# Blocks 2 to 4 of a modulated feed-forward kernel: the first wide product on two levels in all three, modulation taken up early in each second stage, late inner sums on GpSimd

## The chip, the cores and the metric

The kernel runs on one core of one Trainium2 chip. The metric is the device time of one execution in microseconds (us); less is better. Beside it stands a profile: one execution with the start and length of every instruction on the engines TensorE (PE, with its weight loads as PEld), VectorE (DVE), ScalarE (ACT), GpSimd (POOL) and SyncE (SP, which only issues DMAs here).

## The reference, cut to what matters

```python
q_emb = relu(q @ W3 + b3)                      # (64 batches, 512)
v_sum = sum(v, axis=1, keepdims=True)          # v = x: (64, 64, 512)
m = (n * v + v_sum) * q_emb[:, None, :]        # the modulation, n = 64
y = relu(m @ W2 + b2)                          # first wide product, 512 x 512
out = x + (y @ W_base + b_base) + (y @ A_s) @ B_s + routed(y)
# routed: softmax over 6 experts, the best two weigh (y @ A_r) before B_r
```

Everything is float32. There are 4096 rows (64 batches of 64 rows) of 512 features.

## The kernel before

**Tiling.** The rows are cut into four blocks, `k` = 0 to 3 in the code, blocks 1 to 4 in words. A block has 16 batches (1024 rows). Features lie on the 128 partitions in four chunks (`NC` = 4, visited as `CHUNKS` = 0, 2, 1, 3); rows lie along the free axis in two halves of `TB` = 512.

**Stages of a block.** A first stage computes `y` (first wide product, relu). Then come 64 narrow matmuls into `ph` (the low-rank factors and the router, L814), and four `row_sums` of `y` on DVE into the tile `sy`. Then `second` does the second wide product, the gate, the routed part and the output DMAs.

**Wide products with fewer multiplications.** A wide product is a 2 x 2 block product (features by row halves) done with seven half-size products instead of eight (`product`, L168): sums and differences of the weights (`weight_sums`) and of the rows (`row_sums`, L252) go in, and the results are linked by ACT copies from PSUM bank to PSUM bank ("seeds") and by DVE additions. Block 1 does its first product partly directly (`first_mixed`). Block 2 uses seven products on one level (`first_seven`, L429: 14 calls of `product`, of two 128x512 matmuls each). Blocks 3 and 4 use the identity on two levels (`first_inner`, L462): each of the seven outer products is again done with seven inner ones, 49 matmuls of 128x256. For that the inner weight sums `inner_t` (12 DVE instructions, L161 to L164) and the inner row sums of `prepare_inner` are needed: "first" (four of 128x256, outer product 1), "sums" (four of 128x1024, outer products 5, 6, 7, 3) and "late" (four of 128x512, outer products 2 and 4), all on DVE.

**The order inside `first_inner`.** The outer products run as steps t = 0 to 6 in the order (1, 5, 6, 7, 2, 3, 4). `q(n, t)` is the n-th inner matmul of step t. `open_banks(t)` takes two of the six PSUM banks of the pool "pp". `seed_y`, `seed_z` are ACT copies that later matmuls add to; `take_1`, `take_21`, `take_22`, `take_u`, `take_w5` read the banks out, on DVE (L476) or ACT. The additions marked L579 and L582 are done on GpSimd. `q(4, t)` writes the half bank that `take_22(t)` has to have read.

**The modulation.** For each chunk, `sums(c)` on DVE makes `nq` (L203), the sums over the rows (`TENSOR_REDUCE`, L204) and their product with `q` (L205). Then 16 ACT instructions (`batch`, L209) modulate the chunk in place, so 64 a block. This work for block `k + 1` is done during block `k`.

**The queue `behind`.** The program order of each engine is written out by hand; engines run in that order and wait for each other by semaphores. `prepare(k + 1)` lays the modulation, the row sums and the inner sums of the next block into the list `behind` in small units (two `batch` each, some with a DVE step), and `fill(n)` emits the next n units at that point. In `second`, `share()` is called nine times and spreads what is left evenly. The `sums(c)` of block 4 and `inner_t` are made, beside those of block 3, during block 2 (`k == NB - 2` in `prepare`).

Of the kernel before, what the change touches and what calls it, by code (L numbers as in the profile page):

```python
# [19 lines left out]
TB = 512  # L20
# [16 lines left out]
def adaln_ffn(ctx: ExitStack, tc: tile.TileContext, xa, x0, x1, head, w3, w2, wb, a, bcat, br, outT):  # L37
# [155 lines left out]
    def modulate(k):  # L193


        vs[k] = v = xs[k]
        vsum = small.tile([P, NC, BB], F32, tag=f"vsum{k}", name=f"vsum_{k}")
        nq = small.tile([P, NC, BB], F32, tag=f"nq{k}", name=f"nq_{k}")
# [12 lines left out]
        return ({c: lambda c=c: sums(c) for c in CHUNKS},  # L211
                {c: [lambda c=c, b=b: batch(c, b) for b in range(BB)] for c in CHUNKS})
# [62 lines left out]
    modulation = {}  # L275

    def prepare(k):

        if k == NB:
            return
        if k not in modulation:
            modulation[k] = modulate(k)
        sums, batches = modulation[k]
        ss[k], row_steps = row_sums(vs[k], "s")
        early, late = row_steps(slice(0, 1)), row_steps(slice(1, 2))
        units = [] if k == NB - 1 else [[sums[CHUNKS[0]]]]
        for i, c in enumerate(CHUNKS):
            for b in range(0, BB, 2):  # L290
                unit = batches[c][b : b + 2]
                if b == 0 and i + 1 < NC and k < NB - 1:
                    unit.insert(0, sums[CHUNKS[i + 1]])
                if i == NC - 1 and b % 4 == 2:
                    unit.append(early[b // 4])
                units.append(unit)
        if k == NB - 2:
            modulation[k + 1] = modulate(k + 1)
            for n, step in enumerate(list(modulation[k + 1][0].values()) + inner_steps):
                units[1 + n].append(step)  # L300
        behind.extend(units + [[step] for step in late])
        if k > 1:
            behind.extend([step] for step in prepare_inner(k))

    def prepare_inner(k):
# [6 lines left out]

        def late_places():
            late = mid.tile([P, 4, KH, TB], F32, tag="sy", name=f"inner_late_{k}").rearrange("p n k t -> p (n k t)")
            s["late"] = late[:, : 8 * R2].rearrange("p (n o t) -> p n o t", n=4, o=2)
            s["e3"] = late[:, 8 * R2 : 12 * R2].rearrange("p (j t) -> p j t", j=KH)

        def steps(g, a):
            return [
                lambda: nc.vector.tensor_tensor(s[g][:, 0], a(0, 1), a(1, 1), ALU.add),  # L320
                lambda: nc.vector.tensor_tensor(s[g][:, 1], s[g][:, 0], a(0, 0), ALU.subtract),
                lambda: nc.vector.tensor_tensor(s[g][:, 2], a(0, 0), a(0, 1), ALU.subtract),
                lambda: nc.vector.tensor_tensor(s[g][:, 3], a(1, 0), s[g][:, 1], ALU.subtract),
            ]

        late = [late_places] + steps("late", lambda c, r: vs[k][:, KH + c, :, ts(r, R2)])
        where = {1: ("first", 0), 2: ("late", 0), 4: ("late", 1), 5: ("sums", 0), 6: ("sums", 1), 7: ("sums", 2),
                 3: ("sums", 3)}
# [8 lines left out]

        inner[k] = dict(s=side, e3=lambda: s["e3"], late=late)
        first = steps("first", lambda c, r: vs[k][:, c, 0, ts(r, R2)].unsqueeze(1))
# [6 lines left out]
    def first_mixed(y):  # L346
# [81 lines left out]

    def first_seven(k, y):  # L429

        s = ss[k]
        prepare(k + 1)
        pairs = temps(k)
        for j in range(KH):
            f1, f2 = j, KH + j
            bank = lambda n: ps_p.tile([P, TB], F32, tag="pp", name=f"y{n}_{k}_{j}")
            temp = lambda n: pairs[n][:, j]
            px, py, pw, pz = bank("x"), bank("y"), bank("w"), bank("z")
            u, r, r2 = temp("u"), temp("u22"), temp("u12")
            product(px, 1, j, t2, s)  # L440
            nc.scalar.copy(py, px)
            product(pw, 5, j, t2, s)
            nc.scalar.copy(r, pw)
            product(py, 6, j, t2, s, start=False)
            nc.scalar.copy(pz, py)
            product(px, 2, j, t2, s, start=False)
            nc.scalar.copy(u, py)
            fill(2)
            relu(y, f1, 0, px)
            product(pz, 7, j, t2, s, start=False)  # L450
            nc.vector.tensor_tensor(r, pz, r, ALU.add)
            fill(2)
            relu(y, f2, 1, r)
            product(pw, 3, j, t2, s, start=False)
            nc.vector.tensor_tensor(r2, pw, u, ALU.add)
            fill(2)
            relu(y, f2, 0, r2)
            product(pz, 4, j, t2, s, start=False)
            relu(y, f1, 1, pz)
            fill(2)  # L460

    def first_inner(k, y):  # L462


        order = (1, 5, 6, 7, 2, 3, 4)
        for step in inner[k]["late"]:
            step()
        prepare(k + 1)
        t_side, s_side = inner_t, inner[k]["s"]
        pairs, e3 = temps(k), inner[k]["e3"]()  # L470
        p1, p5, u, v7 = (pairs[n] for n in ("u", "u22", "u21", "u12"))
# [84 lines left out]
        take_22(0)  # L556
        q(2, 1)
        for t in range(2, 7):
            open_banks(t)
# [92 lines left out]
    def second(k, y, ph, res):  # L652
# [47 lines left out]

        left = [9]

        def share():
            fill(-(-len(behind) // left[0]))
            left[0] -= 1

# [84 lines left out]
    for k in range(NB):  # L791
        y = mid.tile([P, NC, 2, TB], F32, tag="y", name=f"y_{k}")
        rest = None
        if k == 0:
            first_mixed(y)
        elif k == 1:
            first_seven(k, y)
        else:
            rest = first_inner(k, y)
# [73 lines left out]
```

## Time and profile before

| | |
|---|---|
| median of 3 runs | 263.54 us (263.38 to 265.14) |
| the profiled execution: its time, its span | 263.01 us, 261.2 us |
| granted TensorE clock | 1.0 |
| busy: PE, DVE, ACT, POOL | 98%, 67%, 51%, 6% of the span |

The span goes from the first to the last instruction; some 1.8 us of the profiled execution lie around it. Times below are us from the start of the span. In a listing of instructions in order of time the columns are: start, length, engine, line, operation, output <- inputs, shapes, count, and in brackets the idle time before it with what ended it. Lengths of neighbours can overlap[...]; the distance from start to start is what an instruction costs its queue. The stages stand in time as follows, read from the chain of work that ended last (the chain is 93% PE): first stage of block 1 to 33.66, `ph` and `second` to 72.59; block 2: first stage to 97.52, `ph` to 104.66, `second` to 136.46; block 3: first stage and `ph` to 165.62, `second` to 197.43; block 4: first stage and `ph` to 226.18, `second` to 258.1.

### The profile page before, as it was taken

What the parts mean: (1) busy time and instruction counts of PE and PEld (TensorE: products, weight loads), DVE (VectorE), ACT (ScalarE), POOL (GpSimd) and SP (SyncE); (2) the same over time, 40 slices, a digit from 0 to 9 for tenths busy, and PEclk for the clock granted to TensorE, in tenths of its full rate; (3) what the DMA queues carried; (4) which work ended last, traced back from release to release, by engine and by line L of the source; (5) the groups of instructions that cost most, each with busy time, mean ns of one, the idle gap of its engine ahead of it and who ended that gap; (6) DMA issues with size and microseconds to landing.
All of it is one profiled execution on the core that took longest, in us unless ns stands there. A gap on an engine that the chain in (4) does not pass through costs nothing.

```text
span 261.2 us, 2959 instructions
## 1 busy us (share of the span) xinstructions
PE 255.4 (98%) x962; PEld 156.5 (60%) x962; DVE 175.3 (67%) x335; ACT 133.5 (51%) x355; POOL 16.9 (6%) x25
## 2 busy tenths in 40 slices
PE   7999999999999999999999999999999999999995
PEld 3756895454444349445448889645447889745453
DVE  2895889535975949834997674955599576872332
ACT  2499276579227698356006889647504428112000
POOL 1000000010000000002000250002000070000100
PEclk9999999999999999999999999999999999999999
DMA  6998529403330006000431024300332012500133
GB/s 189 361 345 321 238 73 373 196 3 120 133 142 6 0 8 235 1 1 0 161 123 41 0 80 143 101 0 0 122 120 83 0 61 101 162 0 0 72 141 109
DMA packets 14142, 28.51 MB, mean 109 GB/s; under 512 B 1472, under 2 KB 2496, under 8 KB 14128
## 3 DMA queue, kind: packets, MB, share of 16 engines
q1 hardware_dynamic: 13840, 28.21, 30.4%
q10 hardware_dynamic: 288, 0.13, 0.2%
q8 instruction: 7, 0.11, 0.2%
q14 instruction: 7, 0.06, 0.1%
HBM read 19.94 MB, written 8.39 MB: 108 GB/s over the span
## 4 chain that ended last, share of the span: by engine, by line
PE 93%; ACT 2%; DVE 2%; DMA 2%; SPq 0%; issue 0%; DVEq 0%
PE ph L814 11%; PE ox L170 11%; PE oz L170 11%; PE ow L170 9%; PE ia L485 9%; PE ib L485 7%; PE py L358 5%; PE oy L170 5%; PE ow L677 5%; PE yz L170 3%; PE yw L170 3%; PE ox L677 3%; PE oz L677 3%; PE yy L170 2%; PE yx L170 2%; DMA w_sb<-in_w_dram 2%
## 5 line engine op out<-in xcount | busy, mean ns | idle before, releaser
L209 ACT ACTIVATE x<-x,vsum,nq 128x64 f32<-128x64 f32 x192 | 66.8, 431 | 0.0
L814 PEld LDWEIGHTS ph<-a_sb,y 128*128 128x128 f32 x256 | 29.7, 192 | 1.2 <-issue 0.5
L814 PE MATMUL ph<-a_sb,y 128*128 128x118 f32 x256 | 29.9, 275 | 0.2 <-ACT y L344 0.2
L170 PE MATMUL ox<-y,wb_sb 128*128 128x512 f32 x64 | 29.5, 593 | 0.0
L673 DVE SCALAR_TENSOR_TENSOR xu<-oz,head_sb,xu 128x512 f32<-128x512 f32 x16 | 12.0, 749 | 16.9 <-PE oz L170 14.2
L491 ACT COPY ib<-ia 128x256 f32<-128x256 f32 x14 | 5.0, 360 | 31.0 <-PE ia L485 31.0
L170 PEld LDWEIGHTS ox<-y,wb_sb 128*128 128x128 f32 x64 | 11.9, 190 | 13.4 <-issue 13.4
L344 ACT ACTIVATE y<-u,head_sb 128x256 f32<-128x256 f32 (+1 forms) x26 | 14.4, 600 | 8.4 <-DVE u L417 3.9
L476 DVE TENSOR_TENSOR u<-ib,u 128x256 f32<-128x256 f32 x28 | 11.1, 421 | 9.9 <-PE ib L485 9.9
L741 POOL TENSOR_TENSOR hwd<-hwT 112x512 f32<-112x512 f32 x4 | 5.9, 1464 | 172.5 <-ACT hwT L739 172.5
L358 PE MATMUL py<-v,w_sb 128*128 128x512 f32 (+1 forms) x40 | 14.4, 510 | 1.0 <-DMA w_sb<-in_w_dram 1.0
L170 PE MATMUL oz<-y,tb 128*128 128x512 f32 x32 | 15.1, 592 | 0.0
L170 PE MATMUL oz<-sy,tb 128*128 128x512 f32 x32 | 15.0, 592 | 0.0
L170 PE MATMUL oy<-sy,tb 128*128 128x512 f32 x32 | 15.0, 592 | 0.0
L204 DVE TENSOR_REDUCE vsum<-x 128x16 f32<-128x1024 f32 x12 | 14.5, 1212 | 0.0
L476 DVE TENSOR_TENSOR u<-ia,u 128x256 f32<-128x256 f32 (+1 forms) x24 | 10.8, 464 | 3.7 <-ACT u L523 2.2
L698 DVE TENSOR_TENSOR xu<-ow,xu 128x512 f32<-128x512 f32 x14 | 9.6, 687 | 5.4 <-PE ow L677 5.1
L665 ACT COPY oz<-oy 128x512 f32<-128x512 f32 x8 | 4.6, 570 | 16.9 <-PE oy L170 16.9
L170 PE MATMUL ow<-sy,tb 128*128 128x512 f32 x28 | 13.2, 592 | 0.0
L170 PE MATMUL ow<-sy,wb_sb 128*128 128x512 f32 x28 | 13.2, 591 | 0.0
L673 DVE SCALAR_TENSOR_TENSOR xu<-ox,head_sb,xu 128x512 f32<-128x512 f32 x8 | 6.0, 748 | 10.5 <-PE ox L677 10.5
L247 ACT ACTIVATE v<-x,vsum,nq 128x64 f32<-128x64 f32 x32 | 11.0, 428 | 1.6 <-DVE vsum L245 1.6
(176 smaller groups left out, 435.4 us busy)
## 6 DMA issues: line engine op xcount, KB each, us to landing
xu<-in_x_dram SPq DMA_DIRECT2D x16, 512.0 KB, 4.1
out_dram<-xu SPq DMA_DIRECT2D x30, 256.0 KB, 2.0
x<-in_x_dram SPq DMA_DIRECT2D x12, 512.0 KB, 7.6
x<-in_x_dram SPq DMA_DIRECT2D x7, 256.0 KB, 6.1
w_sb<-in_w_dram SPq DMA_DIRECT2D x4, 256.0 KB, 5.7
wb_sb<-in_wb_dram SPq DMA_DIRECT2D x4, 256.0 KB, 4.9
w_sb<-in_w_dram SPq DMA_DIRECT2D x1, 384.0 KB, 4.5
out_dram<-xu SPq DMA_DIRECT2D x2, 192.0 KB, 1.9
```

Of the source, the lines that this page charges most:

```text
L170: nc.tensor.matmul(ps, w[i][:, c, ts(j, P)], s[i][:, c, :], start=start and c == 0, stop=c == KH - 1, skip_group_check=True,)
L204: nc.vector.tensor_reduce(vsum[:, c, :], xc, AX.XY, ALU.add)
L209: nc.scalar.activation(x, x, AF.Identity, bias=vsum[:, c, b : b + 1], scale=nq[:, c, b : b + 1])
L247: nc.scalar.activation(v[:, c, :, ts(b, NH)], batches_of(c, b, b + 1)[:, :, 0], AF.Identity, bias=vsum[:, c, b : b + 1], scale=nq[:, c, b ...
L344: nc.scalar.activation(y[:, f, h, cols], src, AF.Relu, bias=b2_sb[:, f : f + 1])
L358: nc.tensor.matmul(p[:, :, lo * NH : hi * NH], w2_sb[:, c, ts(f, P)], v[:, c, :, lo * NH : hi * NH], start=(c == 0 and lo == 0), stop=(c = ...
L476: add = lambda o, a, b: nc.vector.tensor_tensor(o, a, b, ALU.add)
L485: nc.tensor.matmul(bank[b, t][:, cols], t_side(o, n), s_side(o, n), start=n == 1, stop=True, skip_group_check=True,)
L673: nc.vector.scalar_tensor_tensor(t, ps[name, j], bb_sb[:, f : f + 1], t, ALU.add, ALU.add)
L677: nc.tensor.matmul(ps[name, j], bcat_sb[:, ts(f, P)], hw, start=False, stop=True, skip_group_check=True)
L698: nc.vector.tensor_tensor(add[:, cols], p[:, cols], add[:, cols], ALU.add)
L814: nc.tensor.matmul(ph[:, h * NS + s, :HC], y[:, c, h, ts(s, P)], a_sb[:, c, :], start=(c == 0), stop=(c == NC - 1),)
```

## The change

`first_seven` is gone, and block 2 also runs `first_inner`. For that, `inner_t` is made earlier: its first four instructions in `first_mixed` between the weight sums and the row sums of block 1, the other eight spread in `behind` of block 1. The four weight sums `tb_steps`, which stood at the head of `behind`, are attached to its first four pairs of modulations, and the first unit is now `sums` of chunk 0. `sums(c)` is cut into two halves of eight batches, with a reduction and a product each, and is no longer made ahead for block 4: for every block it lies at fixed pairs of the queue (halves of the second chunk at pairs 4 and 5, of the third both at 16, of the fourth at 19 and 20). In `second`, `share` takes up the modulation first (4, 5, 6, ... units a call) and the remaining 13 units after it. The "late" inner row sums become eight 128x256 instructions on GpSimd, emitted after the first ten inner matmuls. The "two" ones of them take the place of "first", the "four" ones lie in `sy`. The amount before `second` goes from 6 to 4 units for blocks 2 to 4.

```diff
-        def sums(c):
-            xc = v[:, c].rearrange("p h (b n) -> p b h n", n=NH)
+        def sums(c, half):
+            bs = ts(half, BB // 2)
+            xc = v[:, c].rearrange("p h (b n) -> p b h n", n=NH)[:, bs]
             q = q_sb[:, c, ts(k, BB)]
-            nc.vector.tensor_scalar(nq[:, c], q, float(N), None, ALU.mult)
-            nc.vector.tensor_reduce(vsum[:, c, :], xc, AX.XY, ALU.add)
-            nc.vector.tensor_tensor(vsum[:, c, :], vsum[:, c, :], q, ALU.mult)
+            if half == 0:
+                nc.vector.tensor_scalar(nq[:, c], q, float(N), None, ALU.mult)
+            nc.vector.tensor_reduce(vsum[:, c, bs], xc, AX.XY, ALU.add)
+            nc.vector.tensor_tensor(vsum[:, c, bs], vsum[:, c, bs], q[:, bs], ALU.mult)
...
-    def prepare(k):
+    def prepare(k, also=()):
...
-        units = [] if k == NB - 1 else [[sums[CHUNKS[0]]]]
-        for i, c in enumerate(CHUNKS):
...
-        if k == NB - 2:
-            modulation[k + 1] = modulate(k + 1)
-            for n, step in enumerate(list(modulation[k + 1][0].values()) + inner_steps):
-                units[1 + n].append(step)
-        behind.extend(units + [[step] for step in late])
-        if k > 1:
-            behind.extend([step] for step in prepare_inner(k))
+        c0, c1, c2, c3 = CHUNKS
+        pairs = [batches[c][b : b + 2] for c in CHUNKS for b in range(0, BB, 2)]
+        for places, steps in (((4, 5), sums[c1]), ((16, 16), sums[c2]), ((19, 20), sums[c3]),
+                              ((25, 27, 29, 31), early)):
+            for n, step in zip(places, steps):
+                pairs[n].insert(0, step)
+        for n, step in enumerate(also):
+            pairs[n if n < 4 else 12 + n].append(step)
+        behind.append(sums[c0])
+        behind.extend(pairs)
+        behind.extend([step] for step in late + prepare_inner(k))
...
-        late = [late_places] + steps("late", lambda c, r: vs[k][:, KH + c, :, ts(r, R2)])
+        of = lambda h: lambda c, r: vs[k][:, KH + c, h, ts(r, R2)].unsqueeze(1)
...
+        inner[k] = dict(s=side, e3=lambda: s["e3"], places=late_places,
+                        late=steps("two", of(0), nc.gpsimd) + steps("four", of(1), nc.gpsimd))
...
# first_mixed
-        for step in t2_steps + s_steps():
+        for step in t2_steps + inner_steps[:4] + s_steps():
             step()
-        behind.extend([step] for step in tb_steps)
-        prepare(1)
+        prepare(1, tb_steps + inner_steps[4:])
         fill(1)
...
-    def first_seven(k, y):
...
# first_inner
-        for step in inner[k]["late"]:
-            step()
         prepare(k + 1)
...
         take_22(0)
         q(2, 1)
+        for step in inner[k]["late"]:
+            step()
+        fill(1)
         for t in range(2, 7):
...
# second
-        left = [9]
+        places = list(range(9, 0, -1))
+        most = {9: 4, 8: 5, 7: 6}
         def share():
-            fill(-(-len(behind) // left[0]))
-            left[0] -= 1
+            n = places.pop(0)
+            left = len(behind) - 13
+            fill(min(left, most.get(n, 6)) if left > 0 else -(-len(behind) // n))
...
-        fill(6 if k else 8)
+        fill(4 if k else 8)
```

More of the change, by code (lines that the diff above doesn't have):

```diff
@@ L196, in modulate @@
         vs[k] = v = xs[k]
-        vsum = small.tile([P, NC, BB], F32, tag=f"vsum{k}", name=f"vsum_{k}")
-        nq = small.tile([P, NC, BB], F32, tag=f"nq{k}", name=f"nq_{k}")
-        def sums(c):
-            xc = v[:, c].rearrange("p h (b n) -> p b h n", n=NH)
+        vsum = small.tile([P, NC, BB], F32, tag="vsum", name=f"vsum_{k}")
+        nq = small.tile([P, NC, BB], F32, tag="nq", name=f"nq_{k}")
+        def sums(c, half):
+            bs = ts(half, BB // 2)
+            xc = v[:, c].rearrange("p h (b n) -> p b h n", n=NH)[:, bs]
             q = q_sb[:, c, ts(k, BB)]
-            nc.vector.tensor_scalar(nq[:, c], q, float(N), None, ALU.mult)
-            nc.vector.tensor_reduce(vsum[:, c, :], xc, AX.XY, ALU.add)
-            nc.vector.tensor_tensor(vsum[:, c, :], vsum[:, c, :], q, ALU.mult)
+            if half == 0:
+                nc.vector.tensor_scalar(nq[:, c], q, float(N), None, ALU.mult)
+            nc.vector.tensor_reduce(vsum[:, c, bs], xc, AX.XY, ALU.add)
+            nc.vector.tensor_tensor(vsum[:, c, bs], vsum[:, c, bs], q[:, bs], ALU.mult)
         def batch(c, b):
@@ L209, in batch @@
             nc.scalar.activation(x, x, AF.Identity, bias=vsum[:, c, b : b + 1], scale=nq[:, c, b : b + 1])
-        return ({c: lambda c=c: sums(c) for c in CHUNKS},
+        return ({c: [lambda c=c, n=n: sums(c, n) for n in range(2)] for c in CHUNKS},
                 {c: [lambda c=c, b=b: batch(c, b) for b in range(BB)] for c in CHUNKS})
@@ L273, in fill @@
                 step()
-    modulation = {}
-    def prepare(k):
+    def prepare(k, also=()):
         if k == NB:
             return
-        if k not in modulation:
-            modulation[k] = modulate(k)
-        sums, batches = modulation[k]
+        sums, batches = modulate(k)
         ss[k], row_steps = row_sums(vs[k], "s")
         early, late = row_steps(slice(0, 1)), row_steps(slice(1, 2))
-        units = [] if k == NB - 1 else [[sums[CHUNKS[0]]]]
-        for i, c in enumerate(CHUNKS):
[L290 to L296, printed above, removed]
-        if k == NB - 2:
-            modulation[k + 1] = modulate(k + 1)
-            for n, step in enumerate(list(modulation[k + 1][0].values()) + inner_steps):
-                units[1 + n].append(step)
-        behind.extend(units + [[step] for step in late])
-        if k > 1:
-            behind.extend([step] for step in prepare_inner(k))
+        c0, c1, c2, c3 = CHUNKS
[9 more added lines that the diff above has]
+        behind.extend([step] for step in late + prepare_inner(k))
     def prepare_inner(k):
@@ L313, in late_places, with steps @@
         def late_places():
+            s["two"] = mid.tile([P, 4, 1, R2], F32, tag="inner_s1", name=f"inner_two_{k}")
             late = mid.tile([P, 4, KH, TB], F32, tag="sy", name=f"inner_late_{k}").rearrange("p n k t -> p (n k t)")
-            s["late"] = late[:, : 8 * R2].rearrange("p (n o t) -> p n o t", n=4, o=2)
-            s["e3"] = late[:, 8 * R2 : 12 * R2].rearrange("p (j t) -> p j t", j=KH)
-        def steps(g, a):
+            s["four"] = late[:, : 4 * R2].rearrange("p (n o t) -> p n o t", n=4, o=1)
+            s["e3"] = late[:, 4 * R2 : 8 * R2].rearrange("p (j t) -> p j t", j=KH)
+        def steps(g, a, engine=nc.vector):
             return [
[L320 to L323, printed above, removed]
-            ]
-        late = [late_places] + steps("late", lambda c, r: vs[k][:, KH + c, :, ts(r, R2)])
-        where = {1: ("first", 0), 2: ("late", 0), 4: ("late", 1), 5: ("sums", 0), 6: ("sums", 1), 7: ("sums", 2),
+                lambda: engine.tensor_tensor(s[g][:, 0], a(0, 1), a(1, 1), ALU.add),
+                lambda: engine.tensor_tensor(s[g][:, 1], s[g][:, 0], a(0, 0), ALU.subtract),
+                lambda: engine.tensor_tensor(s[g][:, 2], a(0, 0), a(0, 1), ALU.subtract),
+                lambda: engine.tensor_tensor(s[g][:, 3], a(1, 0), s[g][:, 1], ALU.subtract),
+            ]
+        of = lambda h: lambda c, r: vs[k][:, KH + c, h, ts(r, R2)].unsqueeze(1)
+        where = {1: ("first", 0), 2: ("two", 0), 4: ("four", 0), 5: ("sums", 0), 6: ("sums", 1), 7: ("sums", 2),
                  3: ("sums", 3)}
@@ L336, in side @@
             return s[g][:, {5: 0, 6: 1, 7: 2, 3: 3}[n], i]
-        inner[k] = dict(s=side, e3=lambda: s["e3"], late=late)
+        inner[k] = dict(s=side, e3=lambda: s["e3"], places=late_places,
+                        late=steps("two", of(0), nc.gpsimd) + steps("four", of(1), nc.gpsimd))
         first = steps("first", lambda c, r: vs[k][:, c, 0, ts(r, R2)].unsqueeze(1))
@@ L427, in first_mixed @@
             fill(1)
-    def first_seven(k, y):
[L431 to L460, printed above, removed]
     def first_inner(k, y):
         order = (1, 5, 6, 7, 2, 3, 4)
-        for step in inner[k]["late"]:
-            step()
         prepare(k + 1)
         t_side, s_side = inner_t, inner[k]["s"]
+        inner[k]["places"]()
         pairs, e3 = temps(k), inner[k]["e3"]()
@@ L795, in adaln_ffn @@
             first_mixed(y)
-        elif k == 1:
-            first_seven(k, y)
         else:
```

## The prediction, made before the changed kernel was run

> **What bounds the kernel now.** I read the busy times first, then TensorE by stage, with the stage borders from the chain of waits.
>
> ```profile
> PE 255.4 (98%) x962; PEld 156.5 (60%) x962; DVE 175.3 (67%) x335; ACT 133.5 (51%) x355; POOL 16.9 (6%) x25
> ```
>
> The table by stretches (columns: length, then each engine's busy us and instructions) has in order the first stage of block 2, its `ph`, its `second`, block 3's first stage with `ph`, its `second`, and block 4's first stage with `ph`:
>
> ```profile
> 72.59:97.52 24.93, 24.30 (x59) 10.56 (x58) 17.50 (x37) 17.34 (x41) 0.00 (x0) 1.00 0.09 32
> 97.52:104.66 7.14, 7.14 (x66) 7.14 (x65) 6.45 (x9) 6.03 (x18) 0.00 (x0) 1.00 0.63 222
> 104.66:136.46 31.80, 31.80 (x81) 14.48 (x81) 22.23 (x40) 10.92 (x29) 1.55 (x1) 1.00 0.15 57
> 136.46:165.62 29.16, 29.00 (x163) 25.73 (x163) 20.12 (x41) 24.53 (x70) 5.01 (x4) 1.00 0.24 80
> 165.62:197.43 31.81, 31.81 (x82) 14.49 (x81) 22.46 (x41) 13.23 (x37) 1.77 (x1) 1.00 0.17 62
> 197.43:226.18 28.75, 28.75 (x163) 25.51 (x163) 21.03 (x42) 13.16 (x34) 5.00 (x4) 1.00 0.24 83
> ```
>
> TensorE never rests in `second` (31.80 of 31.80), so nothing can be won there; it can only be lost. A product of two 128x512 matmuls holds it 1.72 us, an inner matmul of 128x256 0.43. So only two things count: how many matmuls there are, and where one waits for DVE, ACT or GpSimd.
>
> **The change part by part.**
>
> *Block 2 on two levels.* Today its first stage and `ph` take 24.93 + 7.14 = 32.07 us (14 x 1.72 = 24.1, and a stall of 0.9 on the seed `yy`). Block 3 does the same on two levels in 29.16, of which 49 x 0.43 + 7.14 = 28.2 is work; about 0.8 is lost at its `ph`, where ACT still has the relus and two modulations to do, which stay in that place. Block 4, with an idle ACT, needs 28.75. Block 2 will have block 3's ACT queue, so I take 29.16: **-2.91**; with 28.75 it would be -3.3.
>
> *`inner_t` in `first_mixed`.* The first four instructions (L161 to L164) cost DVE 2.54 us from start to start in block 2. DVE idles 2.63 there, from 20.4 until the row sums can start at 23.01 (L260 waits for ACT's L247). **0**; if the hole is missed, 0.1. The eight small ones (0.2 to 0.38 each, 2.2 us) lie in block 1's `second`, where DVE has idled over 10 us.
>
> *`sums` of chunk 0 at the head of the queue.* Here the change costs. In order of time, DVE first:
>
> ```profile
> 25.55 0.69 DVE L137 TENSOR_TENSOR tb<-wb_sb 128x512 f32<-128x512 f32 x1
> 26.15 0.42 DVE L413 TENSOR_TENSOR u<-yy,p 128x256 f32<-128x256 f32 x1
> 26.67 0.42 DVE L415 TENSOR_TENSOR u<-yw,u 128x256 f32<-128x256 f32 x1
> ```
> ```profile
> 27.24 1.04 PE L170 MATMUL yw<-s,w_sb 128*128 128x256 f32 x4
> ...
> 31.66 1.13 PE L170 MATMUL yw<-s,w_sb 128*128 128x256 f32 x4
> ```
>
> The matmuls `yw` at 27.24 add to the bank that L415 has just read, and L415 ends at 27.09: only 0.1 of slack. At the second feature chunk L415 ends at 31.60 and `yw` starts at 31.66, 0.2 late, so TensorE does follow it. Now a whole unit stands in L137's place, 0.60 us from start to start: nq 0.08, then twice a reduction 0.72 (128x8, 13.98 to its first dependent at 14.70) and a product 0.09, in all 1.70. L415 ends 1.1 later, at 28.19, and `yw` starts at 28.25: **+1.05**. Nothing gives it back, since TensorE is full up to the end. The other chunk's `yw` has the four `tb` behind it in both orders, so its 0.2 stays. ACT's pairs between the relus (0.34 each from start to start) fit into its idle 0.4 to 1.9 us. The x of block 2 is issued from 14.7 on and its queue runs dry at 23.5, ahead of the reduction at 25.6. The two halves of chunk 1 stand around L425, which then starts at 35.1 instead of 35.27; the row sums of `y` start as before.
>
> *`second` with the modulation early.* In E = its start: `seed_z` of the first half ends at E+5.8, hw and the first output addition on DVE at about E+6.9 (block 3: 171.90 to 172.6), the sums of chunk 2's first half at E+7.7; ACT's eight modulations behind them, 0.34 each, end at E+10.5. The next seed could start at E+10.35 and is needed at E+11.85 (its weight load); it ends at E+11.05. Ten modulations more end at E+14.4; the copies of hwT are due at E+14.65. The last modulation ends at E+20.5 (block 1: E+21.8). DVE's two late row sums, the inner sums and the six outputs then end near E+33.3, 1.5 us into the inner product. Block 3 shows 1.8 today. The last inner sum is read by `q(3, 1)` 6 us in. **0**, with 0.8 us of cover at the tightest place (the second seed). The output DMAs and the four loads of the next rows keep their order on SP.
>
> *"Late" sums off DVE.* In block 4 they hold `take_22(0)` until 202.74, and `q(4, 0)` loads its weights at 202.80, 0.2 to 0.3 late. That goes: **-0.2**. In block 3 `take_22(0)` waited for TensorE anyway. On GpSimd no 128x256 addition is in the trace. L579 takes 1.25 for 128x512, so one takes between 0.63 and 1.25; I take 0.66, half of it and a little start. Eight start when `q(7, 0)` has read "first", 4.2 us into the product (S+4.2), and end at S+9.5 (S+14.2 at the upper price). The first reader, `q(5, 4)`, loads at S+10.3 and needs only the first; `q(5, 6)` loads at S+16. **0.** L579 behind them starts at S+12.1 today.
>
> *`sums` inside the inner product, beside that GpSimd chain.* Blocks 2 and 3 now make chunk 0's sums right after `take_22(0)`. In block 3's times: `take_22(0)` at 140.67, sums 141.01 to 142.71, `take_1(0)`, then `take_22(1)` at 143.05 instead of 142.83, ending at 143.47. `q(4, 1)` reuses that half bank and loads its weights at 144.14, so 0.6 is left. The block of 1.7 us at step 4 delays `take_1(3)` from 149.73 to 151.14; its bank is wanted at 152.3. That is **0** by the rows alone.
>
> Here a rule speaks against the change. The trace shows GpSimd and DVE disturbing each other:
>
> ```profile
> 56.60 1.27 POOL L741 TENSOR_TENSOR hwd<-hwT 112x512 f32<-112x512 f32 x1 [54.88 <-ACT hwT L739]
> ...
> 148.58 2.50 POOL L579 TENSOR_TENSOR inner_late<-u,u 128x512 f32<-128x512 f32 x2 [26.45 <-DVE u L476]
> ...
> 181.43 1.77 POOL L741 TENSOR_TENSOR hwd<-hwT 112x512 f32<-112x512 f32 x1 [27.77 <-ACT hwT L739]
> ```
>
> At 181.43 DVE had just started an addition of two SBUF tiles (L262, 181.40 to 182.08) and the same GpSimd instruction took 0.50 longer. L579, beside DVE additions with one operand in PSUM, took 1.25 apiece. The trace does not show the other direction. The Trainium skill ("SBUF — State Buffer", section "Who interferes with whom") says that a DVE instruction with two SBUF inputs and a GpSimd instruction that reads SBUF exclude each other for the whole instruction, whichever came first. The two tiny products of the sums have two SBUF inputs, and they fall into the chain of eight. By the rows: no loss. By the rule each waits out the GpSimd instruction in progress, 0 to 0.66 us, and nq may too: 0 to 2.0 us on DVE, of which the first 0.6 is covered, so a stall of 0 to 1.5 at `q(4, 1)`, in two blocks. I take about 1.0 us of waiting, 0.4 of stall each: **+0.8**, nearer to the rule, because L741's lengthening is of the rule's kind.
>
> **Sum.** -2.91 + 1.05 - 0.2 + 0.8 = -1.26. Made against the profiled execution (263.01) that is 261.75; against the median of the runs, 263.54, it is 262.3. I say **262.0**, in a range of its own of 261.3 to 262.9. A measurement of this kernel tells about 1%, 2.6 us, from no change, so this counts as no change.
>
> **The rivals.**
>
> *A: GpSimd and the sums don't meet* (their phases miss each other, or DVE isn't held). -2.91 + 1.05 - 0.2 = -2.06, so 261.2. For it: L579's 1.25 beside busy DVE; against it: L741's 0.50.
>
> *B: the lock in full, slower than before.* DVE waits out a whole GpSimd instruction at nq and at both products, 3 x 0.66 = 2.0 us; `take_22(1)` ends at 145.45 instead of 143.47, `q(4, 1)` loads 1.4 late and loses 0.1 of overlap: 1.5 in each of two blocks, -2.06 + 3.0 = +0.9, so 264.2. It decides from 1.6 us of waiting a block (0.6 covered, 1.03 the break-even). If a 128x256 addition costs GpSimd the 1.25 of a 128x512, it is 3.2 a block, +4.4, 267.7. For it: L741; against it: nq and the products are shorter than 0.2 us and a gap between dependent GpSimd instructions may let them in.
>
> *C: the first stage doesn't pay.* If the 1.05 doesn't appear (L415 early enough after all) and block 2 loses as little as block 4: -3.3 - 0.2 + 0 to 0.8, so 259.5 to 260.5. Against it: the `yw` that followed L415 at 31.66.
>
> *D: the early modulation does harm:* the second seed late by more than its 0.8 of cover in three blocks. ACT would have to take 0.44 a modulation instead of 0.34. Up to +1.5 on the sum, 263.5.
>
> **How the numbers follow.** Forecast 0.40, A 0.22, C 0.16, B 0.14, D 0.08. Faster by over 1% (under 260.9): C and a quarter of A, 0.22. Slower by over 1%: most of the upper half of B and half of D, if its mechanism costs more than I found a place for, 0.12. Within 1%: 0.66. The range reaches from C's upper half to B's first price with a little over: 260.0 to 264.8.
>
> **What would show it.** Right: block 2's first stage with `ph` near 29 us for 32.07; `second` at 31.8 in all blocks; block 1's `yw` at 28.3; the vsum products in the inner stage longer than 0.17, or started late beside a GpSimd instruction, and `q(4, 1)` waiting for DVE. Wrong: a `second` above 32 us, a stage of block 2 above 30.5, GpSimd additions above 0.9 us, or `yw` at 27.3.

## The result, and the profile after

| | before | changed |
|---|---|---|
| median | 263.38 us (263.0 to 265.14, 20 runs) | 262.55 us (262.23 to 263.09, 20 runs) |
| ratio | | 0.997, interval 0.996 to 0.9979 |

The gain is 0.83 us, a third of a per cent: for this kernel no change that counts. It was forecast as 262.0 in 260.0 to 264.8.

The page of the changed kernel, first part (busy us, share of the span, instructions):

```profile
PE 255.4 (98%) x1004; PEld 164.6 (63%) x1004; DVE 193.9 (74%) x386; ACT 136.6 (52%) x373; POOL 38.7 (15%) x53
```

PE shows the same 255.4 us as before, now in 42 more instructions, since those of block 2's first stage are half as wide; DVE has 18.6 us more to do and GpSimd 21.8. Sums over the whole span hide what happened, so the stages are next. The table by stretches of the changed kernel has, from the top, `second` of block 1, block 2's first stage with `ph`, its `second`, block 3's two stages, and block 4's first stage with `ph` (columns as in the table of before):

```profile
42.53:74.33 31.80, 31.80 (x81) 14.49 (x81) 28.55 (x58) 15.92 (x44) 1.55 (x1) 1.00 0.37 141
74.33:103.88 29.55, 29.39 (x164) 25.49 (x163) 21.91 (x47) 23.59 (x66) 10.61 (x12) 1.00 0.25 83
103.88:135.93 32.05, 32.05 (x82) 14.41 (x81) 27.74 (x52) 14.06 (x39) 1.50 (x1) 1.00 0.16 58
135.93:165.49 29.56, 29.40 (x164) 25.49 (x163) 21.75 (x47) 23.59 (x66) 10.62 (x12) 1.00 0.25 82
165.49:197.53 32.04, 32.04 (x81) 14.40 (x81) 27.72 (x52) 14.07 (x39) 1.50 (x1) 1.00 0.15 57
197.53:226.10 28.57, 28.57 (x164) 25.58 (x163) 17.73 (x37) 13.16 (x34) 10.61 (x12) 1.00 0.24 83
```

Read the second column against before: block 2 fell from 32.06 to 29.55, but block 3 rose from 29.16 to 29.55, and `second` of blocks 2 and 3 from 31.80 to 32.05. The row of `second` shows PE busy for its whole length, so the loss there is not visible in this table as idle time; it has to be found in the weight loads.

The first stage of block 1 is measured from its first `yy` matmul to the first `ph`: 8.92 us before, 9.80 after.

| stretch | before | changed | difference |
|---|---|---|---|
| first `yy` to first `ph` | 8.92 | 9.80 | +0.88 |
| block 2, first stage and `ph` | 32.06 | 29.55 | -2.51 |
| block 3, first stage and `ph` | 29.16 | 29.55 | +0.39 |
| block 4, first stage and `ph` | 28.75 | 28.57 | -0.18 |
| `second` of block 1, 2, 3 | 31.80, 31.81, 31.80 | 31.80, 32.05, 32.05 | +0.49 |

The sum is -0.93; the medians differ by 0.83. The spans of the two profiled executions are equal, 261.2 us, which seems to contradict both. But the first `yy` starts at 24.57 in the one and at 25.43 in the other. Everything before it is loading, the direct part of block 1 and, in the changed kernel, the four `inner_t` additions. A second profile of the changed kernel (e9, below) settles it.

### The profile page after: what moved, and what is told of

It reads as the page before. It is cut to its first block, busy times and chain, and to the rows that moved or that the text cites. A ratio compares the mean times of both kernels' runs of the same rounds, so it can differ in the third digit from the quotient of the medians.

```text
span 261.2 us, 3176 instructions
## 1 busy us (share of the span) xinstructions
PE 255.4 (98%) x1004; PEld 164.6 (63%) x1004; DVE 193.9 (74%) x386; ACT 136.6 (52%) x373; POOL 38.7 (15%) x53
## 4 chain that ended last, share of the span: by engine, by line
PE 87%; DVE 7%; ACT 2%; DMA 2%; issue 0%; SPq 0%; DVEq 0%
PE ia L446 13%; PE ph L779 11%; PE oz L170 11%; PE ox L170 11%; PE ib L446 10%; PE ow L170 9%; PE oy L170 5%; PE ow L641 5%; PE ox L641 3%; PE oz L641 3%; DMA w_sb<-in_w_dram 2%; DVE vsum L228 1%; PE pt L704 1%; PE last L650 1%; ACT y L340 1%; PE yw L170 1%
## 5 line engine op out<-in xcount | busy, mean ns | idle before, releaser
L212 ACT ACTIVATE x<-x,vsum,nq 128x64 f32<-128x64 f32 x192 | 67.6, 431 | 7.0 <-DVE vsum L208 7.0
L779 PE MATMUL ph<-a_sb,y 128*128 128x118 f32 x256 | 30.5, 276 | 0.3 <-ACT y L340 0.3
L437 DVE TENSOR_TENSOR u<-ib,u 128x256 f32<-128x256 f32 x42 | 16.4, 418 | 18.5 <-PE ib L446 18.3
L452 ACT COPY ib<-ia 128x256 f32<-128x256 f32 x21 | 7.6, 360 | 42.3 <-PE ia L446 42.3
L437 DVE TENSOR_TENSOR u<-ia,u 128x256 f32<-128x256 f32 (+1 forms) x36 | 16.1, 461 | 2.9 <-ACT u L484 1.6
L340 ACT ACTIVATE y<-u,head_sb 128x256 f32<-128x256 f32 (+1 forms) x30 | 15.8, 584 | 4.0 <-DVE u L412 4.0
L446 PE MATMUL ib<-inner_s,inner_t 128*128 128x256 f32 x60 | 17.8, 384 | 0.0
L207 DVE TENSOR_REDUCE vsum<-x 128x8 f32<-128x512 f32 x24 | 16.2, 675 | 0.0
L455 ACT COPY ib<-ib 128x256 f32<-128x256 f32 x21 | 7.6, 363 | 9.9 <-PE ib L446 9.9
L446 PEld LDWEIGHTS ib<-inner_s,inner_t 128*128 128x128 f32 x60 | 11.2, 190 | 2.2 <-ACT ib L455 0.8
```

The source lines that it names most:

```text
L207: nc.vector.tensor_reduce(vsum[:, c, bs], xc, AX.XY, ALU.add)
L340: nc.scalar.activation(y[:, f, h, cols], src, AF.Relu, bias=b2_sb[:, f : f + 1])
L437: add = lambda o, a, b: nc.vector.tensor_tensor(o, a, b, ALU.add)
L446: nc.tensor.matmul(bank[b, t][:, cols], t_side(o, n), s_side(o, n), start=n == 1, stop=True, skip_group_check=True,)
L452: nc.scalar.copy(bank["b", t][:, lo], bank["a", t][:, lo])
L779: nc.tensor.matmul(ph[:, h * NS + s, :HC], y[:, c, h, ts(s, P)], a_sb[:, c, :], start=(c == 0), stop=(c == NC - 1),)
```

## The experiments

All ratios are to the kernel before, run beside each. Line numbers shift a little from kernel to kernel; the names of the tiles tell what is meant. The stage lengths of all runs, in us:

| run | ratio (interval) | `yy` to `ph` | `second` 1, 2, 3 | first stage and `ph`, blocks 2, 3, 4 |
|---|---|---|---|---|
| before | 1 | 8.92 | 31.80 31.81 31.80 | 32.06 29.16 28.75 |
| changed | 0.997 (0.996 to 0.9979) | 9.80 | 31.80 32.05 32.05 | 29.55 29.55 28.57 |
| e1_half_order | 0.9951 (0.9933 to 0.9968) | 9.80 | 31.80 31.80 31.80 | 29.56 29.56 28.57 |
| e2_tb_first | 0.9975 (0.9966 to 0.9985) | 8.72 | 32.29 32.07 32.07 | 30.42 29.56 28.57 |
| e3_sums_moved | 0.9938 (0.9914 to 0.9963) | 9.79 | 31.80 32.07 32.06 | 29.16 29.16 28.58 |
| e4_late_on_dve | 0.996 (0.9948 to 0.9971) | 9.79 | 31.81 32.06 32.06 | 29.46 29.45 28.57 |
| e5_two_levels_alone | 1.0128 (1.0114 to 1.0142) | 8.72 | 31.88 32.42 32.41 | 32.58 30.79 28.76 |
| e7_one_tb_first | 0.9934 (0.992 to 0.9947) | 8.97 | 31.80 32.06 32.05 | 29.57 29.56 28.57 |
| e8_three_mends | 0.9893 (0.9879 to 0.9906) | 8.98 | 31.81 31.81 31.80 | 29.16 29.16 28.57 |
| e9_changed_again | one execution, 262.50 us | 9.80 | 31.81 32.05 32.07 | 29.56 29.56 28.57 |
| e10_even_spread | 0.9961 (0.9947 to 0.9975) | 9.80 | 31.81 32.06 32.05 | 29.56 29.56 28.57 |
| e12_early_in_old_queue | 1.0093 (1.0075 to 1.0112) | 8.72 | 31.88 32.42 32.41 | 32.02 30.59 28.57 |

### e1: the halves of a chunk in order

`pairs[16].insert(0, step)` is called twice for chunk 2, and the second call puts half 1 of the sums *ahead of* half 0. The ACT pair behind them modulates batches 0 and 1, which need half 0. Timeline of the changed kernel, DVE and ACT, and the weight load of TensorE that follows, in `second` of block 2 (starts at 103.88):

```profile
111.52 0.17 DVE L208 TENSOR_TENSOR vsum<-vsum,q_sb 128x8 f32<-128x8 f32 x1
...
112.39 0.17 DVE L208 TENSOR_TENSOR vsum<-vsum,q_sb 128x8 f32<-128x8 f32 x1
...
112.59 2.76 ACT L212 ACTIVATE x<-x,vsum,nq 128x64 f32<-128x64 f32 x8 [2.94 <-DVE vsum L208]
...
115.26 0.57 ACT L629 COPY oz<-oy 128x512 f32<-128x512 f32 x1
...
115.89 0.30 PEld L170 LDWEIGHTS oz<-sy,tb 128*128 128x128 f32 x2 [0.81 <-ACT oz L629]
```

ACT waits for the product at 112.39, not for that at 111.52. Its eight modulations then hold up the copy L629 (the second seed, into the PSUM bank `oz`), and the weight load at 115.89 waits for that seed. The edit:

```diff
-            for n, step in zip(places, steps):
+            for n, step in reversed(list(zip(places, steps))):
                 pairs[n].insert(0, step)
```

> The changed kernel, but the two halves of the third chunk's sums stand in the queue in the order in which ACT needs them (inserting both at pair 16 had put the second half first). Theory 1 (the 0.25 us by which `second` of blocks 2 and 3 is longer than 31.80 is this order: ACT's first modulation waits for the half that is made last, 0.87 us too late, and so does the second seed): `second` of blocks 2 and 3 back at 31.80, PE's wait for the seed gone, about 0.5 us less than the changed kernel in the profile, ratio to before 0.9951. Rival (the seed is late because ten modulations in the fill are too many for ACT, whichever half comes first): 31.9 to 32.05 again, ratio 0.997.

The same place in this run (ACT's modulations, the seed):

```profile
111.17 2.76 ACT L212 ACTIVATE x<-x,vsum,nq 128x64 f32<-128x64 f32 x8 [2.15 <-DVE vsum L208]
...
113.84 0.57 ACT L629 COPY oz<-oy 128x512 f32<-128x512 f32 x1
```

The stage starts 0.6 earlier here, so the modulations begin 0.8 sooner in the stage, and all three `second` are 31.80. The order of the halves is the whole cause of the 0.25 in each of two blocks. Block 1 lays its queue the same way, but takes up eight units instead of four ahead of `second`, and did not lose.

### e2: all four tb at the head of the queue

```diff
-        prepare(1, tb_steps + inner_steps[4:])
+        behind.extend([step] for step in tb_steps)
+        prepare(1, [lambda: None] * 4 + inner_steps[4:])
...
-        fill(4 if k else 8)
+        fill(4 if k else 9)
```

> The changed kernel, but in block 1 the four weight sums of the second product stand again at the head of the queue, ahead of the sums of block 2's chunk 0 (and nine units instead of eight follow the first stage). Theory 1 (the unit of sums in front of L413 costs TensorE 1.05 us at the first matmul `yw` of the third kind): it starts about 0.05 us after the one before it ends, the first stage of block 1 is 0.9 us shorter counted from its row sums, ratio 0.9935 to 0.994, unless the later modulation delays block 2's inner sums. Rival (something else at the start, such as the arrival of the first DMAs, makes block 1 longer): the same distance from the first row sum to `ph`, ratio 0.997.

The first stage gained what was expected, 9.80 to 8.72. But three more units of the queue now come after the start of block 1's `second`, and the 1.08 was more than given back, in two places. TensorE in `second` of block 1, and in the inner product of block 2:

```profile
44.54 1.98 PE L170 MATMUL oy<-sy,tb 128*128 128x512 f32 x4 [0.22 <-ACT oy L630]
```
```profile
81.92 0.70 PE L447 MATMUL ib<-s,inner_t 128*128 128x256 f32 x2 [0.46 <-DVE u L438]
```

`second` of block 1 lost 0.49, block 2's first stage 0.87. So the 1.7 us of sums did cost the first stage its 0.9 to 1.1, but three units more behind it cost as much again; which of them did so was not tried apart.

### e7: only one tb at the head

```diff
+        behind.append(tb_steps[:1])
-        prepare(1, tb_steps + inner_steps[4:])
+        prepare(1, [lambda: None] + tb_steps[1:] + inner_steps[4:])
...
-        fill(4 if k else 8)
+        fill(4 if k else 9)
```

> The changed kernel with one weight sum tb put back at the head of the queue, so that the sums of chunk 0 come after the addition that the next yw waits for, and not ahead of it; one unit more is taken ahead of block 1's second stage, so the modulation is nowhere later. Theory 1 (the place of the 1.7 us of sums alone costs the 1.05): first yy to ph 8.75 us for 9.80, block 1's second stage and block 2 as in the changed kernel (31.8 and 29.55): ratio to the kernel before 0.993, 0.004 under the changed kernel's 0.997. Rival (the second stage has no slack for anything moved behind, as when all four tb stood at the head): the gain comes back as a block 1 second stage of 32.1 or more or a block 2 first stage above 30, ratio 0.996 to 0.998.

0.9934, and nothing is given back: `second` of block 1 is 31.80, block 2 29.57. The additions come at once behind the `tb` (DVE), and the sums after the addition of `yz`:

```profile
25.94 0.69 DVE L137 TENSOR_TENSOR tb<-wb_sb 128x512 f32<-128x512 f32 x1
26.55 0.42 DVE L409 TENSOR_TENSOR u<-yy,p 128x256 f32<-128x256 f32 x1
27.07 0.42 DVE L411 TENSOR_TENSOR u<-yw,u 128x256 f32<-128x256 f32 x1
27.83 0.42 DVE L413 TENSOR_TENSOR u<-yz,u 128x256 f32<-128x256 f32 x1 [0.34 <-PE yz L170]
28.17 0.17 DVE L206 TENSOR_SCALAR nq<-q_sb 128x16 f32<-128x16 f32 x1
```

8.97 is 0.2 above the 8.75 expected. The rest is in this trace: the next addition of `yw` (L417) now stands behind the sums and starts at 29.84, and the weight loads of `yw` at 30.32 and 32.11 wait for DVE's L417 and L411. The matmul starts from there to `ph` come 0.25 us later in all than at their even distance of 0.86.

### e4: the late inner sums on DVE again

```diff
-                        late=steps("two", of(0), nc.gpsimd) + steps("four", of(1), nc.gpsimd))
+                        late=steps("late", lambda c, r: vs[k][:, KH + c, :, ts(r, R2)]))
...
         inner[k]["places"]()
+        for step in inner[k]["late"]:
+            step()
...
-        for step in inner[k]["late"]:
-            step()
         fill(1)
         for t in range(2, 7):
```

> The changed kernel, but the late inner sums are again four DVE instructions of 128x512 at the start of each first stage, as before the change. Theory 1 (the move to GpSimd saves 0.2 us in block 4 and costs about 0.1 us in each of blocks 2 and 3 by the lock on the sums of chunk 0): block 4's first stage with `ph` 28.75 instead of 28.57, blocks 2 and 3 between 29.4 and 29.9, ratio 0.996 to 0.998. Rival (without GpSimd the DVE queue is too full at the start of the inner product: 2.6 us of late sums and 1.7 us of sums of chunk 0 ahead of `take_22(1)`): blocks 2 and 3 30 to 31 us, ratio 0.999 to 1.004.

Two readings. First, blocks 2 and 3 take 29.46 instead of 29.55: with the eight GpSimd additions gone, the sums of chunk 0 run at 0.16 (nq) and 0.17 (product), and that is worth 0.09 a block, not 0.4. Second, a miss: block 4 stays at 28.57. DVE at `take_22(0)` of block 4, here and then in the changed kernel:

```profile
200.81 0.42 DVE L437 TENSOR_TENSOR u<-ib,u 128x256 f32<-128x256 f32 x1 [0.18 <-PE ib L446]
```
```profile
201.74 0.42 DVE L437 TENSOR_TENSOR u<-ib,u 128x256 f32<-128x256 f32 x1 [2.72 <-PE ib L446]
```

In both it waits for TensorE. The late sums are done in time on DVE too, with 0.18 to spare, because the early modulation lets DVE finish the stage before sooner (by 0.96, if one takes the idle time before `take_22(0)` in the next run from that in the changed kernel: 2.72 - 1.76).

### e10: the second stage spread evenly again

```diff
-            n = places.pop(0)
-            left = len(behind) - 13
-            fill(min(left, most.get(n, 6)) if left > 0 else -(-len(behind) // n))
+            fill(-(-len(behind) // left[0]))
+            left[0] -= 1
```

> The changed kernel with the second stage's share() as before: what is left of the queue spread evenly over its nine places. Theory 1 (block 4's 28.57 for 28.75 came from the early modulation, which lets the last row and inner sums end about 1 us sooner, and not from GpSimd): block 4's first stage with ph 28.75 or more, blocks 2 and 3 29.6 to 30.2, second stages 31.8 to 32.05: ratio 0.997 to 1.000. Rival (GpSimd alone is enough for block 4, and the early modulation gains nothing): 28.57 and 29.55 stay, and the second stages fall to 31.8 since ACT has less to do ahead of the second seed: ratio 0.995.

No stage moved by more than 0.01: 28.57 in block 4, 29.56 in blocks 2 and 3, 32.05 in `second`. DVE waited 1.76 us for TensorE ahead of `take_22(0)` in block 4, where it was 2.72 with the early modulation:

```profile
201.37 0.42 DVE L437 TENSOR_TENSOR u<-ib,u 128x256 f32<-128x256 f32 x1 [1.76 <-PE ib L446]
```

With e4 this makes a pair: within the new queue each of the two parts, GpSimd or the early modulation, is enough for 28.57, and the other one only adds cover that nothing uses. No run takes both parts out of the new queue. An estimate: the late sums take 2.54 of DVE's idle time here (2.72 - 0.18), more than the 1.76 left with an even spread, so `take_22(0)` would come some 0.8 late. In the old queue (below) neither part gives 28.76 (e5) and the early modulation alone 28.57 (e12). Neither theory had this whole: theory 1's 28.75 and the rival's `second` of 31.8 both failed. That `second` stays at 32.05 also shows that the early modulation is not what makes the seed late; the order of the halves is.

### e3: the sums ahead of the GpSimd additions

`fill(1)` moves from behind the late steps to the start of `first_inner`, and for blocks 3 and 4's modulation (made in blocks 2 and 3) the first half of chunk 1 moves with it, and the second half goes to pair 3:

```diff
         prepare(k + 1)
+        fill(1)
...
-        for places, steps in (((4, 5), sums[c1]), ...
+        first = sums[c0] + (sums[c1][:1] if k > 1 else [])
+        for places, steps in (((4, 5), sums[c1]) if k == 1 else ((3,), sums[c1][1:]), ...
...
-        behind.append(sums[c0])
+        behind.append(first)
```

> The changed kernel, but for blocks 3 and 4 the sums of chunk 0 and of the first half of chunk 1 are made at the very start of the inner product, before GpSimd starts its eight additions, and the second half of chunk 1 between these eight and the next GpSimd instructions. Theory 1 (GpSimd and the DVE instructions with two SBUF inputs exclude each other; the 0.40 us that blocks 2 and 3 lose against block 3 of before come from that): nq and the products take 0.17 us each time, the stalls of 0.11, 0.16 and 0.13 us in the steps 3 and 6 go, first stage with `ph` 29.15 instead of 29.55 in both blocks, ratio 0.994. Rival (these stalls come from the 1.7 us of sums in the queue themselves, wherever they stand in the inner product): 29.4 to 29.6, ratio 0.997.

29.16 in both blocks, as expected. What was lost there in the changed kernel is seen in its DVE and GpSimd timelines of block 2 and in TensorE's weight loads, in this order (L543 is the L579 of before):

```profile
78.88 0.46 DVE L206 TENSOR_SCALAR nq<-q_sb 128x16 f32<-128x16 f32 x1
...
80.77 0.74 DVE L208 TENSOR_TENSOR vsum<-vsum,q_sb 128x8 f32<-128x8 f32 x1
...
87.42 0.43 DVE L206 TENSOR_SCALAR nq<-q_sb 128x16 f32<-128x16 f32 x1
...
88.47 0.59 DVE L208 TENSOR_TENSOR vsum<-vsum,q_sb 128x8 f32<-128x8 f32 x1
```
```profile
78.58 0.73 POOL L315 TENSOR_TENSOR inner_two<-x 128x256 f32<-128x256 f32 x1 [18.70 <-PE ib L446]
...
80.76 0.73 POOL L318 TENSOR_TENSOR inner_two<-x,inner_two 128x256 f32<-128x256 f32 x1
...
86.55 2.49 POOL L543 TENSOR_TENSOR inner_late<-u,u 128x512 f32<-128x512 f32 x2 [2.19 <-DVE u L437]
```
```profile
82.22 0.30 PEld L446 LDWEIGHTS ib<-s,inner_t 128*128 128x128 f32 x2 [0.24 <-DVE u L437]
...
90.58 0.30 PEld L446 LDWEIGHTS ia<-x,t 128*128 128x128 f32 x2 [0.29 <-DVE u L437]
...
91.57 0.30 PEld L446 LDWEIGHTS ib<-x,inner_t 128*128 128x128 f32 x2 [0.26 <-DVE u L437]
```

Alone these DVE instructions take 0.17. Each long one ends with a GpSimd instruction: 78.88 + 0.46 = 79.34 beside 78.58 + 0.73 = 79.31; 80.77 + 0.74 = 81.51 beside 81.49; 88.47 + 0.59 = 89.06 beside 86.55 + 2.49 = 89.04. The first two, chunk 0's sums, are the ones forecast; they delay `q(4, 1)` (82.22), where TensorE's starts show 0.10 lost. The other two, chunk 1's sums against L543, were not: they delay the additions behind them, and with these `q(1, 6)` (90.58) and `q(4, 4)` (91.57), by about 0.3 in all. In e4 that pair is still held (0.44 and 0.59 there), and its block 2 still stands 0.30 above the 29.16 of e3.

No run separates the holding in this 0.30 from the mere presence of the 1.7 us of sums in that place. The distances speak for the holding: held, the sums take 2.36 us from start to start (87.42 to 89.78), not held 1.67 (chunk 0's in e4), so 0.69 less by estimate. `take_1(3)`, which `q(1, 6)` waits for, ended at 90.53, and the last of the additions ahead of `q(4, 4)` at 91.52; 0.69 sooner, both would have been done before TensorE came, which was held up by 0.15 and 0.10 there.

### e5 and e12: block 2 on two levels in the old queue

From the kernel before: only block 2 goes to `first_inner`, with `inner_t` made earlier. Block 4's sums lose their early place, since that was tied to block 2's queue.

```diff
-        units = [] if k == NB - 1 else [[sums[CHUNKS[0]]]]
+        units = [[sums[CHUNKS[0]]]]
...
-                if b == 0 and i + 1 < NC and k < NB - 1:
+                if b == 0 and i + 1 < NC:
...
-        if k == NB - 2:
-            modulation[k + 1] = modulate(k + 1)
-            for n, step in enumerate(list(modulation[k + 1][0].values()) + inner_steps):
-                units[1 + n].append(step)
+        if k == 1:
+            for n, step in enumerate(inner_steps[4:]):
+                units[17 + n].append(step)
...
-        if k > 1:
-            behind.extend([step] for step in prepare_inner(k))
+        behind.extend([step] for step in prepare_inner(k))
...
-        for step in t2_steps + s_steps():
+        for step in t2_steps + inner_steps[:4] + s_steps():
...
-        elif k == 1:
-            first_seven(k, y)
```

> The kernel before with block 2 on two levels and nothing else of the re-laid queue: sums of a chunk whole, weight sums tb at the head of the queue, late inner sums on VectorE, modulation spread evenly in the second stage. inner_t's first four instructions go into first_mixed, its other eight to units 17 and on of the queue. Theory 1 (the gain is block 2's alone, and what the change lost came with the re-laid queue): first product to ph as before (8.9 us), block 2's first stage with ph 29.2 for 32.06, block 1's second stage 31.8: -2.9, ratio 0.989. Rival (the old queue cannot feed a two-level block 2: with an even spread the modulation ends late, so the inner sums come late): block 2's first stage with ph 30.0 to 31.0 or a second stage above 32.0, ratio 0.993 to 0.998.

Both theories missed: 1.3% *slower*. Block 2 took 32.58, no gain at all on two levels. TensorE, and DVE ahead of the addition that released it:

```profile
79.64 0.70 PE L483 MATMUL ib<-x,inner_t 128*128 128x256 f32 x2 [1.70 <-DVE u L474]
```
```profile
78.56 0.68 DVE L321 TENSOR_TENSOR inner_late<-x,inner_late 128x512 f32<-128x512 f32 x1
79.16 0.42 DVE L474 TENSOR_TENSOR u<-ib,u 128x256 f32<-128x256 f32 x1
```

`take_22(0)` at 79.16 stands behind four inner and four late sums without a gap, and TensorE waits 1.70 us for it. Two more waits follow, of 0.57 (at 84.36) and 0.93 (at 95.48). The first stands behind two whole-chunk sums in a row on DVE (81.48 to 84.31). The second stands behind one more, and there `nq` is held by GpSimd, whose second L580 runs from 91.20 to 92.47:

```profile
91.28 1.22 DVE L203 TENSOR_SCALAR nq<-q_sb 128x16 f32<-128x16 f32 x1
```
```profile
89.97 2.49 POOL L580 TENSOR_TENSOR u<-u,u 128x512 f32<-128x512 f32 x2
```

That is 1.05 longer than the 0.17 it takes alone, so by estimate most of the 0.93 is the holding and not the length of the sums. Block 3 (30.79 for 29.16) and the later second stages (32.4) lost as well. e12 adds the early `share()` to this:

> The run with two levels alone in the old queue (ratio 1.0128; block 2's first stage with ph 32.58, second stages 31.88, 32.42, 32.41, block 3 30.79), with one more part of the change: the early share() of the second stage. Theory 1 (that queue fails because the modulation ends late and the four inner sums with the four late sums stand ahead of take_22(0)): the inner sums end about 1 us sooner, the hole of 1.70 at q(4, 0) shrinks to 0.7 or less, block 2 31.5, block 3 30.2; ratio 1.005 to 1.009. Rival (what fails is the whole-chunk sums of 1.4 us, two in one place, ahead of additions and seeds): the hole changes but the stalls of 0.6 and 0.9 behind it and the second stages of 32.4 stay or grow, ratio 1.010 to 1.014.

The wait of 1.70 fell to 1.16, block 2 to 32.02, block 3 to 30.59; the stalls behind it and the second stages did not move. So theory 1 has the direction, and the rival the greater part, though of the two stalls that stayed the larger (0.92) again has `nq` at 1.22. The rest of the distance to the changed kernel is left to what these runs leave out: GpSimd's late sums, the half-chunk sums at their own places, and the units taken ahead of `second`. They were not tried apart in this queue.

### e8: three mends together, and e9: the changed kernel once more

> Three mends of the changed kernel together: one tb at the head of the queue; the halves of a chunk's sums in order where both stand at one place; in the two-level stage the sums of chunk 0 and half of chunk 1 ahead of the GpSimd additions. Theory 1 (the three losses are separate and add up): yy to ph 8.75, second stages 31.8 in all blocks, first stage with ph 29.16 in blocks 2 and 3: -1.05 - 0.50 - 0.78 = -2.3 against the changed kernel, ratio 0.988. Rival (they share slack, so that what one mend frees another stage eats): ratio 0.991 or more, with a second stage or a first stage of block 2 above these numbers.

The edits are those of e1, e3 and e7. The table by stretches of this run, with block 2's first stage with `ph`, its `second`, and block 3's first stage with `ph` (the lengths of all stages stand in the table of runs):

```profile
72.78:101.94 29.16, 29.00 (x163) 25.73 (x162) 20.91 (x47) 23.60 (x66) 10.62 (x12) 1.00 0.26 86
101.94:133.75 31.81, 31.81 (x83) 14.49 (x82) 27.75 (x52) 14.18 (x39) 1.77 (x1) 1.00 0.15 57
133.75:162.91 29.16, 29.00 (x164) 25.73 (x162) 20.74 (x46) 23.59 (x66) 10.62 (x12) 1.00 0.27 84
```

260.47 us, ratio 0.9893 with 0.9879 to 0.9906. The three losses are separate and their sum holds: 0.82 + 0.49 + 0.79 = 2.1 by the stages, 1.99 by the medians (2.82 under the kernel before, where the changed kernel was 0.83 under it). This version beats both kernels, the one of before by 1.1%, the changed one by about 0.8%. GpSimd's work is unchanged in it (10.62), so the additions cost TensorE nothing here once the small DVE instructions do not fall among them.

> The changed kernel once more, for a second profile. Theory 1 (the late start of its first profile, first yy at 25.43 against 24.57 before, is chance: data landing and first instructions that the change does not touch): yy starts at 24.6 to 25.0 and the span is 260.3 to 260.8, with 9.80 from yy to ph and 29.55 for block 2 as before. Rival (the change itself makes the start late): yy at 25.3 to 25.5 and the span 261.2 again.

The first `yy` came at 24.92, the span was 260.7, and every stage was as in the first profile of the changed kernel. So the same kernel started its first `yy` 0.51 us apart in two executions; in the other runs it lies between 24.56 and 25.32, and the late start at 25.43 is chance. Nor does the change lengthen the way there: from the first direct product (`py`) to the first `yy` it takes 18.68 us in e9 and 18.67 in the kernel before. With the difference of the two starts (0.35) taken off, e9's span is 260.35 against the 261.2 of before: about -0.9, as the stages and the medians say.

## Why the prediction was right

**The sum.** -1.26 was forecast, -0.93 by the stages and -0.83 by the medians came out. The sign holds and the size roughly, and 262.55 lies in the forecast's own range, 261.3 to 262.9. But two terms have another cause or place than I named, and two small ones were missed. One sign of being wrong came true, a `second` above 32 us (32.05 in blocks 2 and 3). That the total still came close is in part luck.

- *Block 2 on two levels, -2.91.* Right: 29.16 is what it takes once the sums are out of its way (e3). The changed kernel has 29.55. One reading on the way was off: of what block 3 of before loses, 0.6 is at its `ph` and 0.3 at two seeds early in the stage, where I put 0.8 at `ph`; the term doesn't depend on it.
- *Sums of chunk 0 at the head, +1.05.* Right in place and mechanism. `yw` waited for DVE's second addition:

```profile
28.60 0.42 DVE L410 TENSOR_TENSOR u<-yw,u 128x256 f32<-128x256 f32 x1
...
29.08 1.13 PE L170 MATMUL yw<-s,w_sb 128*128 128x256 f32 x4 [0.82 <-DVE u L410]
```

  That matmul starts 3.65 us after the first `yy` (29.08 - 25.43) where it started 2.67 after it before (27.24 - 24.57), +0.98 (my own places, 28.25 less 27.24, make 1.01 and not 1.05); by `ph` it is +0.88. The step "so its 0.2 stays" failed: at the second feature chunk `yw` starts at 33.50, 0.86 after `yz`, with nothing late. The 0.2 is missing in e2, e5 and e12 too, which have `tb` at the head as before did and take 8.72; why the one trace of before had it stays open. Against 8.72 the sums cost 1.08, which is the forecast.
- *`inner_t` in the hole, 0.* Right, with nothing to spare: in e5, which has it too, the row sums start at 22.99 and the first `yy` at 24.56, against 23.01 and 24.57 before.
- *Early modulation in `second`, 0.* Wrong by +0.25 in two blocks. The failed step is "the sums of chunk 2's first half at E+7.7; ACT's eight modulations behind them, 0.34 each, end at E+10.5". They ended at 115.35, E+11.5, and the seed at 115.83, E+11.95. I took the two inserts at 16 to keep their order. This is rival D's place (the second seed late), but not its cause: ACT took 0.34 a modulation, as forecast. And e10 shows that "early" has nothing to do with it.
- *Late sums off DVE, -0.2.* Right in size (28.75 to 28.57), half right in cause. In the new queue the move is enough (e10) but not needed (e4); I had not seen that the early modulation does the same.
- *GpSimd and DVE excluding each other, +0.4 in each of two blocks.* Right in mechanism and in sum (+0.39 each, by e3), wrong in place, so the agreement of the sum is luck. At `q(4, 1)`, where I put all of it, there is 0.10 in the trace and 0.09 by e4. The other 0.30 arises later in the stage, where chunk 1's sums meet L543. My step "delays `take_1(3)` from 149.73 to 151.14; its bank is wanted at 152.3" looked at the length of that block of sums, but not at what GpSimd does beside it: in block 2 of the changed kernel `take_1(3)` started 15.4 us into the stage (89.78), where 151.14 would have been 14.7 into block 3 of before. The rule of the Trainium skill ("SBUF — State Buffer", section "Who interferes with whom") was rightly weighed above the row L579: that row had shown GpSimd beside DVE additions with one operand in PSUM, for which the section says that there is no contention. This case agrees: such additions kept their 0.41 to 0.42 beside GpSimd in the changed kernel.

**The rivals.** A (no exclusion) is refuted by 0.17 becoming 0.74. B needed 1.6 us of waiting a block at `q(4, 1)`; there was 0.29 + 0.57 at chunk 0's sums (forecast "about 1.0"), and 0.26 + 0.42 at chunk 1's. The two make 1.54, close to B's 1.6, but they fall on two places, each with cover of its own. C fell with the 0.88. A GpSimd addition of 128x256 took 0.73, against 0.66 taken.

## What to carry to other kernels

When a stage is full on TensorE, replacing matmuls wins at most the time of the matmuls, and the vector work that feeds the new form has to be placed instruction by instruction: here 2.1 of 2.9 us were lost in three kinds of place, each of under 1 us, and the same idea in the old order of work was slower than no change. Ask of every small unit not whether its engine has time, but which addition or seed stands behind it; and when two steps are inserted at one place, look at the order that results. To find such a loss in a stage that shows 100% busy, compare its length with the same stage elsewhere, then read the weight loads.

## What the hardware showed that I had not expected

- The exclusion also holds the smallest instructions, for the whole rest of the other's: nq, with one SBUF operand of 16 elements a partition, took 0.46 for 0.17, and 1.22 in e5 beside a GpSimd addition of 1.27. In e2 an `inner_t` addition of 128x128 took 1.24 for 0.28 beside GpSimd's `hwd` (58.56 to 59.86). In `second` of block 2 of the changed kernel a row sum of 128x512 took 1.76 for 0.69 from 120.50 on, beside `hwd` (120.22 to 121.72), at no cost to TensorE. The reductions between the held instructions kept their 0.67 to 0.68.

```profile
58.77 1.24 DVE L162 TENSOR_TENSOR inner_t<-w_sb,inner_t 128x128 f32<-128x128 f32 x1
```

- On GpSimd half the elements do not cost half: 0.73 for 128x256 where 128x512 takes 1.25.
- The start of a kernel of 263 us varies: the first `yy` came between 24.67 and 25.43 in the changed kernel, its second execution and the seven kernels here whose code up to there is the same. A difference of that size between two profiles is to be read from stages, not from spans.
